# Four graph layers on one core: tokens four to a partition, the adjacency from ScalarE's queue, its square right behind the branch

## The chip, the cores and the metric

The kernel runs on one NeuronCore of a Trainium2 chip. The time is that of one execution on the device, in microseconds; several executions are made and their median is compared. A profiled execution gives, beside its own time, a trace of every instruction on the engines: PE (TensorE, matrix products), DVE (VectorE), ACT (ScalarE), POOL (GpSimd) and SP (which here only issues transfers). PE's instructions write into eight PSUM banks, which the text calls banks; all other tiles of a graph lie in SBUF.

## The reference

There are B = 32 graphs of N = 512 tokens with D = 128 features, and one adjacency matrix of 512 x 512, whose entries are 0 or 1 in the inputs used. Four layers follow each other, each added to its input:

```
for layer in (L0, L1, L2, L3):
    h = relu(layernorm(x))
    x = x + layer(h, adj)

L0: x_h = elu(h Wi + bi); e_ij = sigmoid(tgt_i + src_j + be) * mask_ij
    mask = adj + 0.005 * (adj == 0)
    recv = elu([e x_h, x_h * rowsum(e)] Wn + bn);  [recv, x_h] Wm + bm
L1: five gated steps: m = adj h; z, r = sigmoid(...); c = tanh(...); h = (1-z) h + z c
L2: adj (h W) + bias
L3: sum over k of (adj^k h) W_k, k = 0..3 (the two adjacencies are the same matrix)
```

## The kernel before

A graph's x is held as 128 partitions by four chunks by 128 features: token c*128 + p lies in partition p, chunk c. The tiles that a product with features needs lie the other way, features in the partitions and 512 tokens along the free axis. Float32 products of 512 columns make two passes on PE; products with the adjacency use rounded (float32r) operands, with the token side split into a high and a low part.

The kernel has one prologue and two arms. The prologue loads the adjacency as four row tiles (`A_nat`, loaded at L377 by the helper `load`, whose line L352 the profile shows), and the first graphs (`load_graph`, L369). DVE looks for entries that are neither 0 nor 1 (L551), PE adds up what it found (L566), DVE turns it into an integer `other` (L571), every engine reads it (L1088) and branches (L1089). The inputs used lead to the binary arm, `arm(True)`; the other arm is for any adjacency.

In the prologue PE also transposes the adjacency (L560): bank jc gets the four blocks of column chunk jc, and all four row tiles are operands of each of these operations. In the binary arm ACT makes the layer 0 mask from the banks (L794), POOL compares the mask with 2 to get the rounded transposed adjacency `adjT` (L871), POOL rounds the row tiles into `nat` (L876), and PE makes the square from both (L882), due at 45, which ACT copies out (L887, `adj2T`). PE also makes a permuted adjacency `adjQ` (L920, copied at L923) for the steps of layer 1.

Layer 0 of the first four graphs starts in the prologue. For each: moments on DVE (L513 to L516), a power on POOL (L518), normalising on DVE (L533, graphs 0 to 3), transposes on PE (L410), a copy with relu on ACT (L597), the product with Wi (L481), elu with an exponential (L579) and a tanh (L486) on ACT and a relu on DVE (L584, graphs 0 to 3) or on ACT (L587, all others), two more DVE operations (L589, L591), message and score products (L619), a spread of scores over PE (L656). `aggregated` then forms four masked score tiles (ACT L680, DVE L683), multiplies them with the messages (L691), sums them (pair sums on DVE, L703, and products with ones, L481), multiplies with the node's own features (L732), and makes the products with Wn (L481) and Wm (L742), which is added to x (L501). From graph 4 on transposes go through DRAM (L422, L424, then L435, L440 or L459).

The order of the work is made by a planner at build time. Each operation is listed by `op` with an engine, an assumed duration, a due time and its operands. `Plan.order` steps through time and lets each engine take the ready operation with the earliest due time, if buffers are free; the instructions are then issued in that order, engine by engine. While PE has nothing to do in the first stretch, the planner puts in a filler, a product of ones with ones into a spare bank (L339):

```
plan.idle = Op("PE", 0.224, 0.0, lambda: nc.tensor.matmul(
    spare[:, :P], at(ones), at(ones), start=True, stop=True), False, 0)
plan.idle.known, plan.fill = 0.4, FILL
```

`BRANCH` is the planner's time at which the prologue ends. `nudge` shifts due times by random amounts from a list of seeds, `HEAD_NUDGES`, for operations due before 130. Transfers go out from SP's queue, with the exceptions of accumulating ones from POOL (L719) and the last stores from ACT (L1037).

Of the kernel before, what the change touches and what calls it, by code (L numbers as in the profile page):

```python
# [17 lines left out]
P = 128  # L18
# [6 lines left out]
HEAD_NUDGES = (4000001, 4000006, 4000008, 4000034, 4000054, 4000088, 4000124, 4000206, 4000298, 4000710, 4000778,  # L25
    4000852, 4001301, 4001728, 4002027, 4002029, 4002137, 4002150, 4002536)
# [221 lines left out]
def tile_four_graph_layers(  # L248
# [36 lines left out]
    BRANCH, FILL = 10.0, 50.0  # L285
    MARGIN = 10.0
    FIRST = 4
    ONES = 0

# [26 lines left out]
    def at(v):  # L316
        if v.tile is not None:
            return v.tile
        return places[v.kind][v.slot] if v.whole is None else at(v.whole)[:, v.part]
# [3 lines left out]
    def const(name, shape, dt=F32):  # L323
        if name not in const_tiles:
            const_tiles[name] = cpool.tile(shape, dt, tag=name, name=name)
        return Val(tile=const_tiles[name])

    def chunks(t):
        return t.rearrange("p (c d) -> p c d", c=NC)
# [21 lines left out]
    def load(v, src, due, us=0.5, to=None, earliest=0.0, result=None):  # L351
        op("SP", us, due, lambda: nc.sync.dma_start(at(v) if to is None else to(at(v)), src), [], [v],  # L352
           earliest=earliest, result=result)
        return v
# [13 lines left out]
    def load_graph(b, due, result=None):  # L368
        op("SP", 0.48, due, lambda: nc.sync.dma_start(  # L369
            at(X[b]), x[b].rearrange("(c p) d -> p c d", p=P)),  # L370
            [], [X_group[b // G], X[b]] if b % G == 0 else [X[b]], result=result)
# [4 lines left out]
    for ic, v in enumerate(A_nat):  # L376
        load(v, adj[ts(ic, P), :], -9.5, 0.48, result=2.7 + 0.25 * ic)  # L377
    Wi_sb = load_const(Wi, [P, P], "Wi_sb", -9)
    bi_sb = load_column(bi, "bi_sb", -9)
    load_graph(1, -8.5, 3.2)  # L380
    load_graph(2, -8, 4.0)
# [35 lines left out]
    def by_qci(t):  # L417
        return t.rearrange("p (c q i) -> p q c i", c=NC, i=32)
# [136 lines left out]
    A_turned = [Val("b") for _ in range(NC)]  # L555
    for jc, pt in enumerate(A_turned):
        pt.pieces = True
        def turn(jc=jc, pt=pt):
            for ic in range(NC):
                nc.tensor.transpose(at(pt)[:, ts(ic, P)], at(A_nat[ic])[:, ts(jc, P)], at(ident))  # L560
        op("PE", T_TR, 8, turn, [*A_nat, ident], [pt])
# [39 lines left out]
    def scored(b, hT, due):  # L601
        KEEP = 12
        if b >= G:
# [4 lines left out]
                  relu_by_vector=b < FIRST)  # L608
# [150 lines left out]
    crossing = [*A_turned, *A_nat, *(v for x in begun for v in x[:4])]  # L759
# [13 lines left out]
    def arm(binary):  # L773
        with ExitStack() as stack:
            pool = stack.enter_context(tc.tile_pool(name=f"arm{binary:d}", bufs=1))
            plan.back_to(common)
            plan.slack = 0.3
            plan.free["b"].append((FILL, len(places["b"]) - 1))
            list_rest(binary, pool)
            plan.complete = True  # L780
            if not binary:
                issue(plan.order())
                return
            plan.nudge(0.0, 130.0, HEAD_NUDGES)
            order = plan.order(end=HEAD)
            plan.nudge(TAIL, 2000.0, TAIL_NUDGES)
            issue(order + plan.order())

    def list_rest(binary, pool):
        for v in crossing:  # L790
            v.left -= 1
        for jc, pt in enumerate(A_turned):
            def masked(jc=jc, pt=pt):
                nc.scalar.activation(at(mask)[:, jc, :], at(pt), AF.Identity,  # L794
                                     bias=at(ones)[:, :1], scale=1 / ALPHA - 1)
            if binary:
                op("ACT", T_COPY, 9 + jc, masked, [pt, ones], [mask])
                continue
            z = Val("f")
            op("ACT", T_COPY, 9 + jc, lambda z=z, pt=pt: nc.scalar.mul(at(z), at(pt), 1 / ALPHA), [pt], [z])  # L800
            op("DVE", T_VEC, 9 + jc, lambda jc=jc, z=z, pt=pt: nc.vector.scalar_tensor_tensor(
                at(mask)[:, jc, :], at(pt), 0.0, at(z), op0=ALU.is_equal, op1=ALU.add),
                [pt, z], [mask])
        for b in range(G):
            aggregated(b, begun[b], begin(b))
# [59 lines left out]
        for v in A_nat:  # L865
            if not binary:
                plan.free["f"].append((BRANCH, v.slot))
        if binary:
            adjT = Val(tile=pool.tile([P, NC, N], F32R, tag="AT", name="AT"))
            for jc in range(NC):  # L870
                op("POOL", 0.7, 22, lambda jc=jc: nc.gpsimd.tensor_scalar(  # L871
                    at(adjT)[:, jc, :], at(mask)[:, jc, :], 2.0, None, op0=ALU.is_gt), [mask], [adjT])
            adj2T = Val(tile=pool.tile([P, NC, N], F32R, tag="AA", name="AA"))
            nat = [Val("r") for _ in range(NC)]
            for kc in range(NC):
                op("POOL", 0.62, 24, lambda kc=kc: nc.gpsimd.tensor_copy(  # L876
                    at(nat[kc]), at(A_nat[kc])), [A_nat[kc]], [nat[kc]], earliest=26.0)
            for jc in range(NC):
                pt = Val("b")
                def square(jc=jc, pt=pt):  # L880
                    for kc in range(NC):
                        nc.tensor.matmul(  # L882
                            at(pt), at(nat[kc])[:, ts(jc, P)], at(adjT)[:, kc, :],
                            start=kc == 0, stop=kc == NC - 1,
                        )
                op("PE", NC * T_PASS, 45, square, [*nat, adjT], [pt])
                op("ACT", T_COPY, 45, lambda jc=jc, pt=pt: nc.scalar.copy(  # L887
                    at(adj2T)[:, jc, :], at(pt)), [pt], [adj2T])
        else:
            adjT = Val(tile=pool.tile([P, NC, N], F32, tag="AT", name="AT"))  # L890
            for jc, pt in enumerate(A_turned):
                op("ACT", T_COPY, 9 + jc, lambda jc=jc, pt=pt: nc.scalar.copy(
                    at(adjT)[:, jc, :], at(pt)), [pt], [adjT])
# [24 lines left out]
        for jc in range(NC):  # L918
            pt = Val("b")
            op("PE", T_ADJ, 44, lambda jc=jc, pt=pt: nc.tensor.matmul(  # L920
                at(pt), at(swap), by_qci(at(adjT)[:, jc, :]), start=True, stop=True),
                [adjT, swap], [pt])
            op("ACT", T_COPY, 45, lambda jc=jc, pt=pt: nc.scalar.copy(  # L923
                at(adjQ)[:, jc, :], at(pt)), [pt], [adjQ])
# [104 lines left out]
        def finished(g, ic, pz, d):  # L1029
            xv = X[g * G : (g + 1) * G]  # L1030
            def x_part():
                return at(X_group[g])[:, :, ic, :]
# [3 lines left out]
            def store():  # L1036
                (nc.scalar if g == NG - 1 else nc.sync).dma_start(  # L1037
                    out[g * G : (g + 1) * G, ts(ic, P), :].rearrange("b p d -> p b d"), x_part())
# [52 lines left out]
    with branch.Else():  # L1091
# [4 lines left out]
        out[B - G :, N - P :, :].rearrange("b p d -> p b d"),  # L1096
# [36 lines left out]
```

## Time and profile before

| | |
|---|---|
| median of 3 runs | 1611.24 us (1609.75 to 1612.16) |
| the profiled execution's own time | 1609.89 us |
| its span, first to last instruction | 1608.1 us |
| PE busy | 1599.2 us (99%), 6341 matmul records |
| DVE busy | 1405.8 us (87%) |
| ACT busy | 1120.9 us (70%) |
| POOL busy | 248.0 us (15%) |
| chain that ended last | PE 96% of the span |
| transfers | 188.01 MB, mean 117 GB/s |

A group's line in the profile names the source line, engine, operation, tiles (out<-in), shape and count. In a timeline a row has its start, its length, what it is and how often it follows itself; square brackets tell how long the engine idled before it and what released it. In a table of windows the first number behind the window is its length, and then come each engine's busy time and count, PE's granted clock, the share of the DMA engines and GB/s. A float32 product is two records in the profile (two passes). A busy PE is not always computing at its peak, since the ends of its records are modelled, and a filler counts as busy.

### The profile page before, as it was taken

What the parts mean: (1) busy time and instruction counts of PE and PEld (TensorE: products, weight loads), DVE (VectorE), ACT (ScalarE), POOL (GpSimd) and SP (SyncE); (2) the same over time, 40 slices, a digit from 0 to 9 for tenths busy, and PEclk for the clock granted to TensorE, in tenths of its full rate; (3) what the DMA queues carried; (4) which work ended last, traced back from release to release, by engine and by line L of the source; (5) the groups of instructions that cost most, each with busy time, mean ns of one, the idle gap of its engine ahead of it and who ended that gap; (6) DMA issues with size and microseconds to landing.
All of it is one profiled execution on the core that took longest, in us unless ns stands there. A gap on an engine that the chain in (4) does not pass through costs nothing.

```text
span 1608.1 us, 20921 instructions
## 1 busy us (share of the span) xinstructions
PE 1599.2 (99%) x6341; PEld 1026.2 (64%) x6341; DVE 1405.8 (87%) x3316; ACT 1120.9 (70%) x2119; POOL 248.0 (15%) x248
## 2 busy tenths in 40 slices
PE   9999999999999999999999999999999999999998
PEld 6655555666666666666666666666666666656687
DVE  8899999999898899888898898888998889888862
ACT  5877767886866767667776677676787676665661
POOL 5121011211211111111111111111111101100010
PEclk9999999999999999999999999999999999999999
DMA  3354445444453355453455534454544445333221
GB/s 96 90 148 131 127 111 134 110 123 127 132 149 108 106 125 139 125 135 109 106 138 131 136 94 125 118 145 125 132 127 121 134 116 129 92 92 98 86 60 49
DMA packets 284923, 188.01 MB, mean 117 GB/s; under 512 B 77312, under 2 KB 237952, under 8 KB 284800
## 3 DMA queue, kind: packets, MB, share of 16 engines
q1 hardware_dynamic: 270688, 162.98, 34.3%
q0 software_dynamic: 12528, 22.81, 8.4%
q8 instruction: 52, 0.85, 0.2%
q10 hardware_dynamic: 1584, 0.79, 0.2%
q14 instruction: 71, 0.58, 0.1%
HBM read 82.78 MB, written 73.33 MB: 97 GB/s over the span
## 4 chain that ended last, share of the span: by engine, by line
PE 96%; DVE 1%; DMA 1%; ACT 1%; SPq 0%; issue 0%; POOL 0%; DVEq 0%; ACTq 0%; POOLq 0%
PE b L481 45%; PE b L932 25%; PE b L1007 7%; PE b L691 7%; PE b L1016 4%; PE b L742 4%; PE b L995 2%; PE b L619 2%; PE b L729 1%; DMA f<-m 1%; DMA f<-in_adj_dram 0%; SPq L352 0%; ACT f L527 0%; PE b L882 0%; PE b L410 0%
## 5 line engine op out<-in xcount | busy, mean ns | idle before, releaser
L470 ACT COPY f<-b 128x512 f32<-128x512 f32 x388 | 223.2, 584 | 154.6 <-PE b L932 102.3
L518 POOL TENSOR_TENSOR s<-s,nhalf 128x4 f32<-128x4 f32 x128 | 154.4, 1206 | 975.9 <-DVE s L516 791.4
L932 PE MATMUL b<-AQ,r 128*128 128x512 f32 x1024 | 304.2, 439 | 0.0
L932 PEld LDWEIGHTS b<-AQ,r 128*128 128x128 f32 x1024 | 192.1, 188 | 89.5 <-issue 47.8
L957 DVE TENSOR_TENSOR f<-f,b 128x512 f32<-128x512 f32 x320 | 213.3, 678 | 29.9 <-PE b L481 23.8
L422 DVE STREAM_TRANSPOSE f<-f 128x512 f32<-128x512 f32 x246 | 207.8, 847 | 30.3 <-ACT f L527 29.2
L527 ACT ACTIVATE f<-x,s 128x128 f32<-128x128 f32 x496 | 203.8, 486 | 28.6 <-DVE s L522 28.2
L932 PE MATMUL b<-AT,r 128*128 128x512 f32 x768 | 220.3, 429 | 0.0
L486 ACT ACTIVATE f<-f,b4w 128x512 f32<-128x512 f32 x160 | 115.8, 724 | 118.2 <-DVE f L957 113.5
L932 PEld LDWEIGHTS b<-AT,r 128*128 128x128 f32 x768 | 144.0, 188 | 58.8 <-issue 25.3
L906 DVE TENSOR_TENSOR r<-f,r 128x512 fp32r<-128x512 f32 x224 | 152.3, 682 | 19.2 <-ACT r L902 18.9
L481 PE MATMUL b<-f,u5T 128*128 128x512 f32 x320 | 163.0, 593 | 0.6 <-DVE f L964 0.6
L481 PE MATMUL b<-f,u3T 128*128 128x512 f32 x320 | 163.4, 592 | 0.0
L481 PE MATMUL b<-f,w4T 128*128 128x512 f32 x320 | 163.1, 592 | 0.0
L481 PE MATMUL b<-f,w3T 128*128 128x512 f32 x320 | 163.1, 592 | 0.0
L481 PE MATMUL b<-f,w5T 128*128 128x512 f32 x320 | 162.7, 592 | 0.0
L902 ACT CAST r<-f 128x512 fp32r<-128x512 f32 x224 | 137.7, 619 | 18.5 <-DMA f<-m 18.0
L486 ACT ACTIVATE f<-b,b5w 128x512 f32<-128x512 f32 x160 | 109.3, 684 | 48.9 <-PE b L481 46.5
L486 ACT ACTIVATE f<-f,b3w 128x512 f32<-128x512 f32 x160 | 115.2, 721 | 34.5 <-DVE f L957 33.6
L974 DVE TENSOR_TENSOR f<-f,f 128x512 f32<-128x512 f32 x160 | 109.0, 682 | 28.8 <-ACT f L486 28.7
L1007 PEld LDWEIGHTS b<-V,f 128*128 128x128 f32 x1024 | 122.6, 192 | 15.1 <-issue 12.9
L719 POOL DMA_DIRECT2D f<-f x87 | 77.8, 894 | 344.7 <-DVE f L957 37.3
(114 smaller groups left out, 2379.1 us busy)
## 6 DMA issues: line engine op xcount, KB each, us to landing
m<-f SPq DMA_DIRECT2D x246, 256.0 KB, 2.2
f<-m SPq DMA_DIRECT2D x186, 256.0 KB, 2.9
f<-f POOLq DMA_DIRECT2D x87, 256.0 KB, 3.6
f<-m SPq DMA_DIRECT2D x240, 64.0 KB, 2.4
x<-in_x_dram SPq DMA_DIRECT2D x32, 256.0 KB, 3.3
f<-f SPq DMA_DIRECT2D x29, 256.0 KB, 2.3
f<-d SPq DMA_DIRECT2D x28, 256.0 KB, 5.6
out_dram<-x SPq DMA_DIRECT2D x28, 256.0 KB, 2.4
```

The lines of the kernel that those rows point to most:

```text
L422: op("DVE", us, due, lambda: nc.vector.transpose(view_out(at(blocks)), view_in(at(src))), [src], [blocks])
L470: op("ACT", us, due, lambda: nc.scalar.copy(at(t), at(src)), [src], [t])
L481: nc.tensor.matmul(to, at(w), of, start=start, stop=stop)
L486: op("ACT", us, due, lambda: nc.scalar.activation(at(dst), at(src), AF.Tanh, bias=at(bias), scale=scale), [src, bias], [dst])
L518: op("POOL", 1.2, due, lambda: nc.gpsimd.tensor_tensor(stat(SCALE), stat(VAR), at(neg_half), op=ALU.pow), [s, neg_half], [s], two=False)
L527: nc.scalar.activation(at(h)[:, ts(c, P)], at(X[b])[:, c, :], AF.Relu, bias=stat(SHIFT)[:, c : c + 1], scale=stat(SCALE)[:, c : c + 1],)
L691: op("PE", T_MM, d, lambda jc=jc: nc.tensor.matmul(at(pn), at(msg)[:, ts(jc, P)], at(es[jc]), start=jc == 0, stop=False), [msg, es[jc]], [pn])
L902: op("ACT", T_COPY, due, lambda: nc.scalar.copy(part(hi), whole()), [src], [hi], keep=1)
L906: op("DVE", T_VEC, due, lambda: nc.vector.tensor_tensor(part(lo), whole(), part(hi).bitcast(F32), op=ALU.subtract), [src, hi], [lo], two=two)
L932: nc.tensor.matmul(at(pa), at(part)[:, ts(jc, P)], view(at(columns)[:, jc, :]), start=jc == n == 0, stop=jc == NC - 1 and n == PARTS - 1,)
L957: op("DVE", T_VEC, d, lambda: nc.vector.tensor_tensor(at(s), at(u), at(pg), op=ALU.add), [u, pg], [s])
L1007: nc.tensor.matmul(at(pz)[:, ts(i, D)], at(t[i])[:, ts(ic, P)], at(V[k]), start=i == n == 0, stop=last and i == G - 1 and n == len(terms) - 1,
```

## The change

Tokens are placed four to a partition: token 4p + c lies in partition p, chunk c. The loads of x read 2048 contiguous bytes a partition instead of four pieces of 512; the stores of the result write pieces of 512 bytes, 2048 apart. Row tile c of the adjacency is rows 4p + c, and its columns are taken with stride 4 (`by_token`) wherever a chunk of columns is read. Sums over tokens, the mask and the squares are in the same new order throughout.

The adjacency's four loads are issued by ACT ahead of its table load. Each row tile is now transposed as soon as it is there, into all four banks (`adjacency_turned`), ahead of the branch. ACT rounds the row tiles into `nat` (four `q` buffers) and copies the banks into the rounded `adj_r`, also ahead of the branch; the mask comes from `adj_r` behind it. POOL's eight operations (L871, L876) are gone. The 16 matmuls of the square are listed one by one, due at 12, and so are planned right behind the branch. Relu of graphs 2 and 3 goes from DVE to ACT. `BRANCH` is 9, the planner adds 0.3 (PE) or 0.75 (others) for the branch itself, and there is a new list of nudges. The other arm transposes the adjacency again for itself.

```diff
-    BRANCH, FILL = 10.0, 50.0
+    BRANCH, FILL = 9.0, 50.0
+    SQUARE, NAT = 12.0, 0.0
+    BRANCHES = 0.75
+    A_LANDS = (3.0, 3.3, 3.6, 3.8)
...
-            at(X[b]), x[b].rearrange("(c p) d -> p c d", p=P)),
+            at(X[b]), x[b].rearrange("(p c) d -> p c d", c=NC)),
...
-        load(v, adj[ts(ic, P), :], -9.5, 0.48, result=2.7 + 0.25 * ic)
+        load(v, adj.rearrange("(p c) n -> c p n", c=NC)[ic], -9.5, 0.45, result=A_LANDS[ic], eng="ACT")
...
-        op("PE", T_TR, 8, turn, [*A_nat, ident], [pt])
+    def by_token(v):
+        return at(v).rearrange("p (t c) -> p c t", c=NC)
+
+    def adjacency_turned(due):
+        banks = [Val("b") for _ in range(NC)]
+        for pt in banks:
+            pt.pieces = True
+        for ic in range(NC):
+            def turn(ic=ic):
+                for jc, pt in enumerate(banks):
+                    nc.tensor.transpose(at(pt)[:, ts(ic, P)], by_token(A_nat[ic])[:, jc, :], at(ident))
+            op("PE", T_TR, due + ic, turn, [A_nat[ic], ident], banks)
+        return banks
+
+    adj_r = const("adj_r", [P, NC, N], F32R)
...
+    nat = [Val("q") for _ in range(NC)]
+    for jc, pt in enumerate(adjacency_turned(-1)):
+        op("ACT", T_COPY, NAT + jc, lambda jc=jc: nc.scalar.copy(chunks(at(nat[jc])), by_token(A_nat[jc])), [A_nat[jc]], [nat[jc]])
+        op("ACT", T_COPY, jc, lambda jc=jc, pt=pt: nc.scalar.copy(at(adj_rows[jc]), at(pt)),
+           [pt], [adj_rows[jc], adj_r])
...
-                  relu_by_vector=b < FIRST)
+                  relu_by_vector=b < 2)
...
-                op("POOL", 0.7, 22, lambda jc=jc: nc.gpsimd.tensor_scalar(
-                    at(adjT)[:, jc, :], at(mask)[:, jc, :], 2.0, None, op0=ALU.is_gt), [mask], [adjT])
...
-                op("POOL", 0.62, 24, lambda kc=kc: nc.gpsimd.tensor_copy(
-                    at(nat[kc]), at(A_nat[kc])), [A_nat[kc]], [nat[kc]], earliest=26.0)
...
-                op("PE", NC * T_PASS, 45, square, [*nat, adjT], [pt])
...
+            for n in range(NC * NC):
+                kc, jc = divmod(n, NC) if SPLIT else divmod(n, NC)[::-1]
+                op("PE", T_PASS, SQUARE, lambda jc=jc, kc=kc, pt=squares[jc]: nc.tensor.matmul(
+                    at(pt), at(nat[kc])[:, ts(jc, P)], at(rows[kc]), start=kc == 0, stop=kc == NC - 1),
+                    [nat[kc], rows[kc]], [squares[jc]])
...
-                    out[g * G : (g + 1) * G, ts(ic, P), :].rearrange("b p d -> p b d"), x_part())
+                    out[g * G : (g + 1) * G].rearrange("b (p c) d -> c p b d", c=NC)[ic], x_part())
```

## The prediction

> **What bounds the kernel now.** I read the page first, then the windows, then the timelines and the chain of the first 40 us. The page gives PE 1599.2 of 1608.1 us busy, and the chain puts 96% on PE. The windows show where PE is not busy, and how near DVE comes to it:
>
> ```profile
> core 0: us, PE busy (x) PEld busy (x) DVE busy (x) ACT busy (x) POOL busy (x), PEclk, DMA share, GB/s
> 0.00:10.00 10.00, 8.33 (x59) 7.69 (x59) 5.71 (x26) 1.68 (x3) 2.64 (x10) 1.00 0.77 219
> 10.00:20.00 10.00, 8.94 (x63) 7.15 (x62) 8.14 (x39) 7.40 (x13) 8.67 (x10) 1.00 0.53 138
> 20.00:30.00 10.00, 9.99 (x53) 6.46 (x52) 9.97 (x27) 6.72 (x16) 7.81 (x11) 1.00 0.10 26
> 30.00:40.00 10.00, 9.82 (x41) 5.69 (x40) 9.12 (x29) 7.14 (x15) 1.39 (x1) 1.00 0.01 2
> 40.00:130.00 90.00, 90.00 (x354) 55.37 (x353) 80.51 (x182) 71.22 (x138) 19.34 (x23) 1.00 0.44 116
> 130.00:400.00 270.00, 270.00 (x944) 162.06 (x943) 255.46 (x588) 202.93 (x379) 38.46 (x37) 1.00 0.45 124
> ```
>
> From 40 us on PE never stops, so time can be won only before. There it idles 1.67 + 1.06 + 0.01 + 0.18 = 2.92 us, and much of what counts as busy is the filler matmul of L339, which computes nothing. Windows of L339 alone:
>
> ```profile
> core 0: us, PE busy (x) PEld busy (x), PEclk, DMA share, GB/s
> 0.00:12.00 12.00, 6.73 (x40) 6.54 (x41) 1.00 0.72 202
> 12.00:20.00 8.00, 3.34 (x30) 3.17 (x29) 1.00 0.54 143
> 20.00:30.00 10.00, 3.03 (x22) 2.64 (x22) 1.00 0.10 26
> ```
>
> Filler 13.10 us and idle 2.92 us: PE loses 16.0 us of its first 40. The timelines say what it waits for (PE, then DVE, then POOL):
>
> ```profile
> 6.31 0.42 PE L560 MATMUL b<-ident,f 128*128 128x128 f32 x2
> 7.06 0.33 PE L560 MATMUL b<-ident,f 128*128 128x128 f32 x1 [0.33 <-DMA f<-in_adj_dram]
> 7.69 1.64 PE L560 MATMUL b<-ident,f 128*128 128x128 f32 x13 [0.30 <-DMA f<-in_adj_dram]
> ...
> 11.42 3.06 PE L339 MATMUL b<-ones 128*128 128x128 f32 x26
> ...
> 17.95 0.33 PE L825 MATMUL b<-ident,f 128*128 128x128 f32 x1 [1.06 <-DMA b4u<-in_L_gnn_u_b_dram]
> ```
>
> ```profile
> 24.03 1.89 DVE L683 SCALAR_TENSOR_TENSOR f<-f,mask 128x512 f32<-128x512 f32 x3
> 25.84 1.09 DVE L703 TENSOR_TENSOR f<-f,f 128x512 f32<-128x512 f32 x1
> ...
> 26.99 0.96 DVE L683 SCALAR_TENSOR_TENSOR f<-f,mask 128x512 f32<-128x512 f32 x1
> ```
>
> ```profile
> 25.57 3.87 POOL L876 CAST r<-f 128x512 fp32r<-128x512 f32 x4
> ```
>
> The adjacency tiles land one by one to 7.65; then comes the branch, then a filler stretch; from 20 us DVE is full. Under POOL's casts one DVE operation takes 0.96 to 1.09 instead of the 0.63 between the three at 24.03.
>
> **The change, part by part.** PE's useful work is the same: in the binary arm the changed program has the same transposes, squares (16), permutations (4) and products. Fillers fall from 18 ahead of the branch and 26 behind it to 17 and 17. The last 2010 rows of PE's built order are equal in both, so the end of the run is untouched. The sum is therefore what PE loses in its first 40 us.
>
> *Loads.* Four adjacency loads leave SP (1.91 us of issuing) for ACT's queue and go out at 0.72 to 2.6 instead of 1.23 to 3.15. ACT's table load (1.28 us) and the warm-up stand behind them and end near 4.1, before ACT's first tile: hidden. Wi, bi and graph 1 go out 2 us earlier; graph 2 now waits in SP's queue for the first adjacency tile, graph 3 for the third, behind them bias and Wm loads. First users: DVE near 11.0 and 17; x loads land 2.8 to 5.1 us after their issue near 4.3 and 6.3, so both are covered. When does the last adjacency tile land? Low: 7.65 less 0.6 of earlier issue less the 256 KB of graph 0 no longer ahead in its queue (0.88 us at the 291 GB/s of 5 to 10 us): 6.1. High: all of x0, Wi, the adjacency and graph 1 (1.64 MB) before it on the curve of before (147 GB/s to 5 us, then 291): 8.1. I take the middle, 7.0, having no nearer row.
>
> *PE up to the branch.* Seven fillers (14 passes) at 0.208 (19 passes took 3.96 us up to 5 us): 1.04 to 3.95. Then four transposes per tile as it lands (13 took 1.64) and one filler, to 7.0. Idle there: 7.05 − 3.95 − 12 × 0.126 − 0.24 = 1.35. After the last transposes five fillers (to 8.6), the count, three fillers, the transposes of graph 0, one filler; the register read and compare (0.58) hides behind a filler of 0.2 where it hid behind a product before: 0.4 idle.
>
> *ACT ahead of the branch* has two times four new 512-column casts. Three of the strided ones fall between landings, the fourth ends 7.6, the four PSUM copies (0.545 each: three L923 took 1.64) end 9.85, and its branch 10.45 (11.36 before). Queued behind them is graph 0's copy (L597): 11.05, so its product starts at 11.75 instead of 10.51; graph 1's copy goes from 14.96 to 15.1. That cost is covered by the squares: all 16 (0.23 each, 3.7 us) now stand there instead of fillers, and leave 33.8 and 43.9, where PE had other work anyway. If the rounded tiles come late, that cover is gone and PE idles one for one. Strided reading has no ACT row; low 0.62 (L902, contiguous), high 0.62 × 1.18/0.668 = 1.09 (slowest over fastest of DVE's L422, which reads contiguous or with stride 4). At 1.09 the branch of ACT comes 1.15 later. I take 0.62, the row of the same engine.
>
> *POOL* loses 4 × 1.49 (L871) and 3.87 (L876): 9.8 us. Its powers for graphs 1 and 2 come about 1 us sooner, and DVE runs at 0.6 to 0.68 between 24 and 30. *DVE* loses two relus (0.66 each) to ACT (0.58 each, in its gaps).
>
> *DVE's chain*, from 7.0, by spacings in the timeline (moments 1.26, normalising 1.03, a 512-column operation 0.60 to 0.66): counts to 7.75, graph 0 normalised 8.85, branch 11.0, graph 1 normalised 13.35, relu 14.0, graph 2 normalised 16.35, then masks and pair sums of graph 0 from 21.6 to 25.2, and its own-sum product (L732) at 27.7 where before has 31.73. Normalising graph 3 (1.03) stood before it and now stands behind it: 3.0 ahead. PE by the built order meets these at 22.5 (first L691), 28.65 (Wn) and 33.9 (Wm), each 0.2 to 0.6 behind its operand; one wait of 0.3 at graph 3's transposes.
>
> *Sum on PE:* start 1.04; fillers 14 × 0.208 + 54 × 0.118 (26 took 3.06) = 9.3; tiles 1.35; branch 0.4; other waits and hops 0.6: 12.7 against 16.0. Three pair-sum products stretched 0.18 to 0.25 by the late DVE (1.04, 1.11 and 1.10 in the chain for 0.86) go as well: 0.5 net. Gain 3.3 + 0.5 = **3.8 us**. The L825 wait (1.06) is in the 16.0; the weights are issued 1.5 us sooner and needed at 16.1, about when they land.
>
> *Output rows* keep 512-byte pieces but lie apart. The last store took 3.1 us to land. Bounds: 0, and 0.7 (f<-m 2.9 against m<-f 2.2 us). I take 0, as the pieces keep their size. Loads of x in larger pieces and all other stores lie under a DMA share of 0.36 to 0.47.
>
> **A rule against the change.** The row first: L339 takes 0.208 us a pass up to 5 us and 0.118 after 11 us, while PEclk shows 1.00 throughout. The Trainium skill, "TensorE: Matmul & The Clock Gate", Part 1, says PE starts at half rate and is released only after a window of some 3.4 us of sustained work. The changed PE pauses between 4 and 7 us; by that rule it could stay slow to about 8.3, and transposes and five fillers would take up to 1.5 us more: gain 2.3. I keep the sum by the rows, because the pauses are short.
>
> The Trainium skill, "SBUF — State Buffer", section "Door 1: The DMA port swizzle", says that an access which goes to a new 16-byte line each time pays; stride-4 float32 reads do that. No row here shows it for PE or ACT.
>
> **Rivals.** (1) *The start does not move enough.* Last tile at 8.1 (1.1 lost) and strided casts at 1.09 (0.7 of the 1.15 passes the squares' slack): gain 2.0, 1609.2. For it: tiles spaced 0.63 with 0.95 or more DMA share; against it: no 512-byte pieces ahead of them. (2) *Slower: the new order between about 45 and 860 us puts PE behind a turned tile.* m<-f lands after 2.2 us and f<-m after 2.9; a trip that nothing covers costs 5.1. It decides once 7.0 us are lost, so one trip in full and part of another; two give 1607.4 + 10.2 = 1617.6. For it: DVE is 255.46 of 270 busy there, so late work is caught up slowly. Against it: PE idled 0 us from 40 to 400 and 0.65 from 400 to 800, and 14.5 us of DVE idle are left. (3) *More:* last tile at 6.1, no hops, rows as above: 0.9 + 0.6, and the stretched products in full (0.2): gain 5.5, 1605.7.
>
> **How the numbers follow.** The profiled execution took 1609.89 (span 1608.1, 1.8 around it), 1.35 below the median of 1611.24. Less 3.8: 1606.1 for such an execution, **1607.4** for a median. A measurement tells 0.2%, 3.2 us, from no change: faster is below 1608.0. Forecast with case (3): 0.62. Rival 1, within 0.2%: 0.24. Rival 2: 0.14. The forecast's own range is 1605 to 1608. The range asked for goes below case (3) by the 1.2 that runs spread about their median (1604.5). Above, it takes in rival 1 with the store's 0.7 and the casts' other 0.45 (1610.4), and a third of one uncovered trip (1.6): 1612. The rest of rival 2 stays out.
>
> **What the next profile would show.** Right: fillers x68 and some 9.3 us; last adjacency transposes near 7.1; Wi's first product near 11.8 among the squares; no POOL casts, and mask products on DVE at 0.6 to 0.7; L732's first near 27.7; PE without idle from 35 us; the last 0.7 ms alike. Wrong: transposes or casts of stride 4 twice as long; a last tile after 8; PE idle above 2 us between 45 and 860; a landing of the last store above 3.8 us.

## The result, and the profile after

| | before | after |
|---|---|---|
| median | 1611.34 us (1609.75 to 1613.97, 8 runs) | 1606.47 us (1605.23 to 1609.74, 8 runs) |
| the profiled execution's own time | 1609.89 us | 1605.48 us |
| its span | 1608.1 us | 1603.6 us |

The ratio is 0.997, with a 95% interval of 0.9959 to 0.9981: 4.9 us less, where 3.9 (1611.34 less the forecast 1607.4) was forecast. The profiled executions are 4.5 us of span apart.

The windows of the changed kernel, with the columns of the first table of before (length; PE, PE's weight loads, DVE, ACT, POOL busy; clock; DMA share; GB/s):

```profile
0.00:10.00 10.00, 7.77 (x51) 7.11 (x51) 5.04 (x22) 6.62 (x8) 3.21 (x12) 1.00 0.75 242
10.00:20.00 10.00, 10.00 (x59) 8.14 (x60) 8.18 (x37) 9.70 (x21) 3.24 (x6) 1.00 0.53 136
20.00:30.00 10.00, 9.80 (x43) 5.83 (x43) 9.93 (x33) 7.97 (x18) 3.37 (x4) 1.00 0.02 6
30.00:40.00 10.00, 10.00 (x65) 7.75 (x64) 9.86 (x28) 9.95 (x23) 1.11 (x1) 1.00 0.17 55
...
130.00:400.00 270.00, 270.00 (x946) 162.29 (x945) 254.54 (x585) 202.37 (x380) 39.99 (x36) 1.00 0.46 125
400.00:800.00 400.00, 400.00 (x1581) 256.65 (x1580) 360.18 (x858) 287.23 (x547) 62.82 (x58) 1.00 0.46 124
```

PE idles 2.23 us in the first 10 and 0.20 in the next 30; before it was 1.67 and 1.25. The wait of 1.06 for a bias of layer 1 is gone. ACT, which was 1.68 busy up to 10 us, is 6.62 busy there and 9.70 in the next ten: it carries the new casts. The fillers alone (L339 before is L347 here; PE and PE's weight loads):

```profile
0.00:12.00 12.00, 6.34 (x34) 5.62 (x34) 1.00 0.64 202
12.00:20.00 8.00, 0.75 (x6) 0.82 (x7) 1.00 0.64 168
20.00:30.00 10.00, 1.70 (x14) 1.50 (x13) 1.00 0.02 6
30.00:40.00 10.00, 2.44 (x16) 2.10 (x16) 1.00 0.17 55
```

They are 68 passes with 11.2 us of records, against 88 with 13.1 (the windows count a record that lies across a bound twice, so their counts add up to 70 and 92). Nearly all that went stood between 12 and 20 us (3.34 before, 0.75 now), where the square now is; new ones stand behind 30 us. The timeline of PE shows the exchange:

```profile
4.98 0.96 PE L574 MATMUL b<-ident,f 128*128 128x128 f32 x4 [0.58 <-DMA f<-in_adj_dram]
...
7.86 0.75 PE L574 MATMUL b<-ident,f 128*128 128x128 f32 x4 [0.61 <-DMA f<-in_adj_dram]
8.44 1.28 PE L347 MATMUL b<-ones 128*128 128x128 f32 x10
...
11.13 0.39 PE L347 MATMUL b<-ones 128*128 128x128 f32 x2
11.27 1.41 PE L906 MATMUL b<-adj_r,q 128*128 128x512 f32 x5
12.52 1.02 PE L490 MATMUL b<-f,Wi_sb 128*128 128x512 f32 x2
12.97 2.42 PE L906 MATMUL b<-adj_r,q 128*128 128x512 f32 x8
...
23.60 3.10 PE L715 MATMUL b<-f,f 128*128 128x512 f32 x6 [0.18 <-DVE f L707]
```

L906 is the square; its last three passes end at 16.4. The row at 11.13 also shows how a sum of records misleads: the group of two fillers is 0.39 long, but the next row starts 0.14 behind its start, since the modelled end of a pass lies over the start of the next. Short groups are overstated in this way. So the losses are counted below from one PE start to the next: a filler with its whole distance, every other pass with what it takes beyond its usual distance (0.228 for a pass with the adjacency, 0.429 for a 512-column float32 pass, 0.109 to 0.112 for 128 columns). The undisturbed work is 1576.5 us in every kernel here, so the losses make up the whole difference:

| profiled execution | median us | lost on PE in the first 50 us | later | behind the last start |
|---|---|---|---|---|
| before | 1611.3 | 17.0 | 9.0 | 5.6 |
| after | 1606.5 | 13.8 | 7.9 | 5.5 |
| e1_sp_queue | 1607.1 | 14.0 | 12.0 | 5.6 |
| e2_tokens_back | 1607.4 | 13.6 | 8.6 | 5.6 |
| e4_square_late | 1616.6 | 17.1 | 14.5 | 5.6 |
| e5_weights_strided | 1606.7 | 14.5 | 8.7 | 5.6 |
| e6_no_fill8 | 1605.6 | 13.1 | 8.7 | 5.6 |
| e8_no_fill8_weights | 1605.7 | 13.5 | 8.0 | 5.5 |
| e7_before_act_casts | 1612.3 | 16.7 | 10.3 | 5.5 |
| e9_no_nudges | 1610.5 | 16.6 | 9.6 | 5.6 |
| e10_before_no_nudges | 1616.8 | 17.9 | 11.9 | 5.6 |

Of the 4.5 us between the two profiled spans 3.2 lie in the first 50 us, 1.1 later and 0.1 at the end. By place, PE loses 3.8 us less between 10 and 20 us and 1.1 less between 20 and 30, but 0.4 more before 10 and 1.2 more between 30 and 40: part of what the square gave comes back as fillers where it used to stand. DVE and ACT of the changed kernel at the start:

```profile
22.77 2.49 DVE L707 SCALAR_TENSOR_TENSOR f<-f,mask 128x512 f32<-128x512 f32 x4
25.18 1.29 DVE L727 TENSOR_TENSOR f<-f,f 128x512 f32<-128x512 f32 x2
...
28.84 0.68 DVE L756 TENSOR_TENSOR f<-f,b 128x512 f32<-128x512 f32 x1
```

```profile
4.87 4.32 ACT L583 CAST q<-f 128x512 fp32r<-128x512 f32 x4 [0.74 <-DMA f<-in_adj_dram]
9.08 2.04 ACT L584 CAST adj_r<-b 128x512 fp32r<-128x512 f32 x4
11.33 0.60 ACT L621 ACTIVATE f<-b 128x512 f32<-128x512 f32 x1 [0.21 <-PE b L419]
```

The four strided casts take 4.32, or 1.08 each, and fill ACT without a gap from the first tile to 9.1, when the copies of the banks start. The product of the node's own features on DVE (L756, L732 before) starts at 28.84 where before has 31.73.

### The profile page after: what moved, and what is told of

Its sections match the earlier page's. It is cut to its first block, busy times and chain, and to the rows that moved or that the text cites. A ratio compares the mean times of both kernels' runs of the same rounds, so it can differ in the third digit from the quotient of the medians.

```text
span 1603.6 us, 20898 instructions
## 1 busy us (share of the span) xinstructions
PE 1596.1 (100%) x6321; PEld 1024.3 (64%) x6321; DVE 1404.7 (88%) x3314; ACT 1130.4 (70%) x2129; POOL 240.3 (15%) x240
## 4 chain that ended last, share of the span: by engine, by line
PE 99%; DMA 0%; DVE 0%; ACTq 0%; issue 0%
PE b L490 46%; PE b L950 26%; PE b L1025 7%; PE b L715 7%; PE b L1034 4%; PE b L766 4%; PE b L643 2%; PE b L1013 2%; PE b L753 1%; DMA f<-in_adj_dram 0%; PE b L419 0%; PE b L347 0%; PE b L906 0%; ACTq L361 0%; PE b L680 0%; DVE s L522 0%
## 5 line engine op out<-in xcount | busy, mean ns | idle before, releaser
L536 ACT ACTIVATE f<-x,s 128x128 f32<-128x128 f32 x496 | 203.8, 487 | 27.7 <-DVE s L531 27.3
L950 PE MATMUL b<-adj_r,r 128*128 128x512 f32 x768 | 220.8, 430 | 0.0
L950 PEld LDWEIGHTS b<-adj_r,r 128*128 128x128 f32 x768 | 143.8, 188 | 59.2 <-issue 27.3
L924 DVE TENSOR_TENSOR r<-f,r 128x512 fp32r<-128x512 f32 x224 | 152.5, 683 | 13.1 <-ACT r L920 12.7
L920 ACT CAST r<-f 128x512 fp32r<-128x512 f32 x224 | 137.7, 619 | 12.3 <-DMA f<-m 11.9
L1025 PEld LDWEIGHTS b<-V,f 128*128 128x128 f32 x1024 | 122.7, 192 | 14.8 <-issue 12.7
```

The costliest lines, as they stand in the source:

```text
L536: nc.scalar.activation(at(h)[:, ts(c, P)], at(X[b])[:, c, :], AF.Relu, bias=stat(SHIFT)[:, c : c + 1], scale=stat(SCALE)[:, c : c + 1],)
L920: op("ACT", T_COPY, due, lambda: nc.scalar.copy(part(hi), whole()), [src], [hi], keep=1)
L924: op("DVE", T_VEC, due, lambda: nc.vector.tensor_tensor(part(lo), whole(), part(hi).bitcast(F32), op=ALU.subtract), [src, hi], [lo], two=two)
L950: nc.tensor.matmul(at(pa), at(part)[:, ts(jc, P)], view(at(columns)[:, jc, :]), start=jc == n == 0, stop=jc == NC - 1 and n == PARTS - 1,)
L1025: nc.tensor.matmul(at(pz)[:, ts(i, D)], at(t[i])[:, ts(ic, P)], at(V[k]), start=i == n == 0, stop=last and i == G - 1 and n == len(terms) - 1,
```

## The experiments

Each is the changed kernel with one edit, or with two where the heading says so; two runs start from the kernel before, as their headings say. Times of the kernel before beside them: 1611.59 us (20 runs) for the first four, 1611.76 (21 runs) for the next four and 1612.47 (10 runs) for the last.

### The adjacency from SP's queue again

```diff
-        queue = nc.sync if eng == "SP" else nc.scalar
+        queue = nc.sync
```

> The changed kernel with its four adjacency loads issued from SP's queue, interleaved with x, Wi, bi; the order of PE, DVE and POOL is unchanged. Theory A (tiles arrive as fast as the transfer engines bring everything that was asked for, whichever queue asks): the last tile lands within 0.5 us of the 7.81 of the changed kernel, time within 1 us of it. Theory B (a queue of its own brings the adjacency earlier): the last tile, issued near 3.6 instead of 2.14, lands at 9 or later, and the time rises by 1 to 1.5 us.

Measured: 1607.07 us (1606.16 to 1609.98, 7 runs), ratio 0.9974 [0.9963, 0.9985]. The last tile's transposes on PE:

```profile
8.16 0.75 PE L574 MATMUL b<-ident,f 128*128 128x128 f32 x4 [0.75 <-DMA f<-in_adj_dram]
```

They start 0.3 us later than from ACT's queue (7.86), and the start loses 0.2 more. That is all that the queue does; the median is 0.6 above the changed kernel's, inside both intervals.

This profiled execution took 1609.93, though. Its later losses are 4.1 us above those of the changed kernel, and nearly all of them come from one wait, in an order that ran without it in the other program. The waits of PE, then windows around it (PE, its weight loads, DVE, ACT, POOL; clock; DMA share; GB/s):

```profile
PE b L490 <- DVE f L982: 2.3, 1, 2.3
```

```profile
526.00:528.50 2.50, 1.01 (x3) 0.53 (x4) 2.50 (x5) 1.20 (x2) 0.88 (x1) 1.00 0.81 133
528.50:532.00 3.50, 3.50 (x10) 2.73 (x9) 1.18 (x4) 3.22 (x8) 0.86 (x1) 0.51 0.83 212
```

PE waits 2.33 us for DVE, and then its granted clock is 0.51 over the next 3.5 us. The clock record itself has 0.5 from 528.58 to 531.99, 3.41 us. Of the run's times, 1608.26, 1609.93 and 1609.98 stand apart from the other four (1606.16 to 1607.07), and the changed kernel has one such time too (1609.74). The mean granted clock on record is 0.998 for that one and for the three longest of the next experiment (1610.31 to 1610.71), and 0.999 or 1.000 for all others of these two kernels; the long ones of this experiment have 0.999 and 1.000, like the short ones. So lost clock goes with some of them, and what made the others long is open.

### Tokens and tiles in the old order

```diff
-            at(X[b]), x[b].rearrange("(p c) d -> p c d", c=NC)),
+            at(X[b]), x[b].rearrange("(c p) d -> p c d", p=P)),
...
-        load(v, adj.rearrange("(p c) n -> c p n", c=NC)[ic], -9.5, 0.45, result=A_LANDS[ic], eng="ACT")
+        load(v, adj[ts(ic, P), :], -9.5, 0.45, result=A_LANDS[ic], eng="ACT")
...
-        return at(v).rearrange("p (t c) -> p c t", c=NC)
+        return at(v).rearrange("p (c t) -> p c t", c=NC)
...
-                    out[g * G : (g + 1) * G].rearrange("b (p c) d -> c p b d", c=NC)[ic], x_part())
+                    out[g * G : (g + 1) * G, ts(ic, P), :].rearrange("b p d -> p b d"), x_part())
```

The last store, written apart at the end, is changed in the same way.

> The changed kernel with tokens in the old order: x in pieces of 512 bytes again, no reading with stride 4, stores as before. The order of all engines is unchanged. Theory A (stride-4 reading is what ACT's casts of 1.08 us pay, and larger pieces of x earn nothing that shows): casts take 0.6, ACT's copy of graph 0 comes 0.5 to 1.5 us sooner than 11.33, time 0.3 to 1 us below the changed kernel. Theory B (the larger pieces bring the first tiles sooner, and lighter loads help through the run): casts 0.6, but the last tile lands after 8.5, time 1 us or more above the changed kernel.

Measured: 1607.43 us (1606.03 to 1610.71, 11 runs), ratio 0.9978 [0.9969, 0.9987]. On ACT:

```profile
7.64 0.62 ACT L583 CAST q<-f 128x512 fp32r<-128x512 f32 x1 [0.30 <-DMA f<-in_adj_dram]
...
11.04 0.60 ACT L621 ACTIVATE f<-b 128x512 f32<-128x512 f32 x1 [0.83 <-PE b L419]
```

A cast takes 0.62 again, and a warm transpose 0.109 us a pass instead of 0.120. The casts keep pace with the tiles, and ACT now waits 0.83 for PE's transposes of graph 0, so its copy comes only 0.29 sooner. The time is not lower (the interval holds the changed kernel's ratio). So the order of the tokens has a price in single instructions and none that can be measured in the sum; the larger pieces of the loads and the stores at a distance show no effect either (5.6 and 5.5 us behind the last start of PE).

### The square not before 33

```diff
-                    [nat[kc], rows[kc]], [squares[jc]])
+                    [nat[kc], rows[kc]], [squares[jc]], earliest=33.0)
```

> The changed kernel with the 16 matmuls of the square not allowed before the planner's 33 us; the planner fills the gap with fillers and orders the rest anew. Theory A (the gain is that the square, 3.7 us of PE, stands where fillers stood): PE's loss in the first 40 us rises from 13.7 to 16 to 17.5, time 2.5 to 3.7 us above the changed kernel, about as the kernel before. Theory B (the gain is the earlier start and the freer DVE; the square would be done in some other gap): time within 1 us of the changed kernel.

Measured: 1616.56 us (1615.3 to 1616.87, 7 runs), ratio 1.0029 [1.0018, 1.0041]. The fillers alone:

```profile
12.00:20.00 8.00, 3.26 (x26) 3.04 (x25) 1.00 0.51 143
```

Between 12 and 20 us there are 3.26 us of them again, as before the change, and the start loses 17.1 us: the whole gain of the start (3.2) is gone. So the square behind the branch is what it rests on. The time overshoots, since the planner then makes another order for what follows. The waits of PE that are longest behind 40 us:

```profile
PE b L715 <- DVE f L707: 1.7, 2, 1.3
...
PE b L950 <- DVE r L924: 1.0, 1, 1.0
...
PE b L766 <- DVE f L615: 1.0, 1, 1.0
```

The longest of L707's (1.3) is at 99 us, the other two at 1583 and 1364 us. PE loses 14.5 us behind 50 us instead of 7.9. The run therefore shows the head's worth by its place in the trace, not by its time.

### The stride on the weights of the square, not on ACT's cast

```diff
-        op("ACT", T_COPY, NAT + jc, lambda jc=jc: nc.scalar.copy(chunks(at(nat[jc])), by_token(A_nat[jc])), [A_nat[jc]], [nat[jc]])
+        op("ACT", T_COPY, NAT + jc, lambda jc=jc: nc.scalar.copy(at(nat[jc]), at(A_nat[jc])), [A_nat[jc]], [nat[jc]])
...
-                    at(pt), at(nat[kc])[:, ts(jc, P)], at(rows[kc]), start=kc == 0, stop=kc == NC - 1),
+                    at(pt), by_token(nat[kc])[:, jc, :], at(rows[kc]), start=kc == 0, stop=kc == NC - 1),
```

> The changed kernel with ACT's four casts of the adjacency reading in order, and stride 4 moved into PE's weight reads of the square; all orders unchanged. Theory A (stride 4 costs ACT 0.5 us a cast, and ACT ahead of the branch holds up graph 0): casts 0.6, ACT's copy of graph 0 0.4 to 1.2 us sooner than 11.33, time 0.3 to 1 us lower. Theory B (the landing and the branch hold it up, or weight reads pay instead): time the same within 0.3 us, or higher.

Measured: 1606.66 us (1605.98 to 1608.06, 6 runs), ratio 0.997 [0.9958, 0.9982]. The casts take 0.62, but PE is the later one now. PE, then ACT:

```profile
6.35 2.66 PE L574 MATMUL b<-ident,f 128*128 128x128 f32 x12
```

```profile
11.74 0.60 ACT L621 ACTIVATE f<-b 128x512 f32<-128x512 f32 x1 [1.16 <-PE b L419]
```

ACT waits 1.16 us for the transposes of graph 0 and copies them 0.4 later than in the changed kernel. In this execution PE's passes keep a distance of 0.213 up to 8.75, so twelve transposes take 2.66; and fillers stand ahead of L419. So this run alone doesn't tell what the slow cast costs. The changed kernel does: there too the copy waits for PE behind the slow casts, by 0.21 us, and without the stride (the second experiment) it came only 0.29 sooner.

The stride has its price at the new place too. The weight loads of the square, here and in the changed kernel:

```profile
L906 PEld LDWEIGHTS b<-adj_r,q x16: 307/310/329, 11.7 to 16.6; 128*128 128x128 f32 x16
```

```profile
L906 PEld LDWEIGHTS b<-adj_r,q x16: 187/188/192, 11.2 to 15.9; 128*128 128x128 f32 x16
```

A load takes 0.31 us for 0.19 (shortest, median and longest in ns), and the 16 passes take 4.58 us from start to start, where they took 4.29. That is 0.3 of the 0.7 us which the start loses more than in the changed kernel; the rest goes with the slow passes (0.213) up to 8.75.

### Without the fillers ahead of the branch

```diff
-    plan.idle = Op("PE", 0.224, 0.0, lambda: nc.tensor.matmul(
-        spare[:, :P], at(ones), at(ones), start=True, stop=True), False, 0)
+    fillers = []
+    def filler():
+        fillers.append(len(fillers))
+        if not 8 <= fillers[-1] < 16:
+            nc.tensor.matmul(spare[:, :P], at(ones), at(ones), start=True, stop=True)
+    plan.idle = Op("PE", 0.224, 0.0, filler, False, 0)
```

The plan is the same; the five fillers ahead of the count and the three ahead of graph 0's transposes aren't issued (lines move by 4).

> The changed kernel without the five fillers ahead of the count and the three ahead of graph 0's transposes; all else in the same order. Theory A (ACT's eight casts, which end at 11.1, hold up graph 0, the fillers only pass the time): graph 0's copy on ACT moves from 11.33 by 0.3 us at most, PE's loss stays within 0.4 of 13.8, time within 0.5 us of the changed kernel. Theory B (the fillers hold up the count, the branch and graph 0's transposes, 1.1 us each): DVE's branch and all behind it 0.5 to 1 us sooner, time 0.5 to 1 us lower. If PE then pauses long enough to stay at half rate, its passes are 0.21 beyond 9 us and the loss grows instead.

Measured: 1605.63 us (1605.43 to 1606.37, 5 runs), ratio 0.9963 [0.9949, 0.9977]. ACT, then DVE:

```profile
10.79 0.63 ACT L625 ACTIVATE f<-b 128x512 f32<-128x512 f32 x1
```

```profile
22.13 2.49 DVE L711 SCALAR_TENSOR_TENSOR f<-f,mask 128x512 f32<-128x512 f32 x4
...
28.21 0.68 DVE L760 TENSOR_TENSOR f<-f,b 128x512 f32<-128x512 f32 x1
```

Graph 0's copy is 0.54 sooner, and with it the masks (22.13 for 22.77) and the own-feature product (28.21 for 28.84): fillers ahead of the branch do delay what DVE does 12 us later (the last tile landed at 7.66 here, so up to 0.15 of it can be that). The start loses 13.1 instead of 13.8. The median is the lowest of all, 0.8 below the changed kernel's, but with overlapping intervals.

### Both of these

The two edits above together.

> The changed kernel without those eight fillers, and with ACT's casts reading in order (stride 4 in PE's weight reads). Theory A (casts and fillers hold up graph 0 together, so only both taken away show): graph 0's copy on ACT near 10.4 to 10.8 instead of 11.33, its product near 11.4, PE's loss 12.5 to 13.3, time 0.4 to 1.2 us below the changed kernel. Theory B (DVE, whose branch comes at 12, holds up all that counts): copy sooner, but the first mask product on DVE stays within 0.3 of 22.8 and the time within 0.3 us.

Measured: 1605.71 us (1604.68 to 1607.28, 5 runs), ratio 0.9963 [0.995, 0.9977]. PE, then ACT:

```profile
6.35 2.76 PE L578 MATMUL b<-ident,f 128*128 128x128 f32 x12
```

```profile
10.62 0.60 ACT L625 ACTIVATE f<-b 128x512 f32<-128x512 f32 x1
```

Nothing is added: with neither fillers nor slow casts in the way the copy is 0.17 sooner than without the fillers alone, and the start loses 13.5 instead of 13.1. The square with strided weights has 0.3 of this (4.62 us for 4.30); the rest goes with PE's passes, which kept the long distance of 0.213 up to 10.6 us in this execution (up to 6.9 in the other).

### The kernel before, with POOL's four row casts on ACT

```diff
-                op("POOL", 0.62, 24, lambda kc=kc: nc.gpsimd.tensor_copy(
+                op("POOL", 0.62, 24, lambda kc=kc: nc.scalar.copy(
```

The plan's order stays; only the engine that makes the cast differs.

> The kernel before with the four casts of POOL between 25.6 and 29.4 done by ACT, which idles there; all other orders unchanged. Theory A (POOL's casts slow DVE): the mask products and pair sums there take 0.6 to 0.7 instead of 0.96 to 1.09, the first L732 moves from 31.73 to 30.0 to 30.8, PE's loss from 17.0 to 16.0 to 16.7, time 0.3 to 1 us below the kernel before. Theory B (DVE is slow there for another reason): they stay at 0.9 or more and the time within 0.3 us.

Measured: 1612.29 us (1609.55 to 1613.04, 11 runs), ratio 0.9998 [0.9989, 1.0007]. DVE:

```profile
26.34 0.68 DVE L703 TENSOR_TENSOR f<-f,f 128x512 f32<-128x512 f32 x1
27.07 0.68 DVE L683 SCALAR_TENSOR_TENSOR f<-f,mask 128x512 f32<-128x512 f32 x1
...
30.84 0.68 DVE L732 TENSOR_TENSOR f<-f,b 128x512 f32<-128x512 f32 x1
```

The same operations took 0.96 to 1.09 while POOL cast. So the casts on POOL were what slowed DVE, and without them its chain is 0.9 sooner (30.84 for 31.73). PE gains by it where it meets DVE: between 24 and 37 us its passes other than fillers lose 0.28 us beyond their usual distances, where they lost 1.15. But in all the start loses 16.7 instead of 17.0, since in this execution the wait for the bias of layer 1 is 1.30 instead of 1.06 and the fillers take 0.3 more at the start. The median shows no gain.

### No list of nudges, in the changed kernel and in the one before

```diff
-HEAD_NUDGES = (7100000, 7100078, 7100153, 7100154, 7100740, 7100413, 7100768, 7100794, 7100559, 7100664, 7100595,
...
-    7100950, 7100955, 7100970, 7100973)
+HEAD_NUDGES = ()
```

> The changed kernel with an empty list of nudges; the planner orders the rest by itself. Theory A (the list earns time behind the head too: without it PE stalls that the changed kernel doesn't have): PE's loss in the first 50 us within 1.5 of 13.8, stalls after it 2 to 8 us more, time 2 to 9 us above. Theory B (only the head counts): time within 1.5 us of the changed kernel.

Measured: 1610.49 us (1609.91 to 1611.58, 10 runs), ratio 0.9994 [0.9985, 1.0003]. Without its own list the changed kernel takes as long as the one before with its list; the start loses 16.6, and 9.6 follow later. The list is worth 2.8 us in the start and 1.7 behind it. Neither of the two theories had put it there to that extent. What it doesn't tell is what the old structure takes without its list; the same edit on the kernel before:

> The kernel before, with its list of nudges emptied, as the changed kernel was run without its own (that took 1610.5 us; with the list 1606.5). It says what the structure of the change is worth when neither program has a searched order. Theory A: the structure gives the start its gain, and the lists only keep the order of each program clean; the kernel before loses some 4 us without its list too: 1614 to 1617 us, and the changed program is 4 us or more ahead list for list. Theory B: the structure is worth little by itself, and the new list found what the old one did not: 1611 to 1612 us, about the time with the list, and at most 1.5 us behind the changed program without nudges. In the profile, A has more than 17 us lost by PE in its first 50 us (before: 17.0; the changed program without nudges: 16.6) or new stalls behind 40 us; B has 17 us and no new stalls.

Measured: 1616.82 us (1613.57 to 1619.68, 6 runs), ratio 1.0031 [1.0019, 1.0043]. That is theory A: the old kernel also falls back without a list, by some 4.4 us, and list for list the change keeps its worth: 0.9994 over 1.0031 is 0.9963, some 6 us, where it is 0.997 with the lists. The start loses 17.9, later 11.9. The waits of PE, and a window (columns as above):

```profile
PE b L480 <- DMA f<-m: 2.6, 1, 2.6
PE b L480 <- DVE f L731: 1.1, 2, 0.8
```

```profile
1200.00:1500.00 300.00, 296.66 (x1090) 183.24 (x1089) 258.65 (x561) 200.90 (x367) 35.15 (x33) 1.00 0.39 106
```

The largest is a product that waits 2.6 us for a turned tile, the mechanism of rival 2, in another program. Without lists the start differs by only 1.2 us and what follows by 2.3 (in profiled executions, of which that of the kernel before was its fastest). By place, the changed program still loses far less between 10 and 20 us (1.3 against 6.4), but 4.4 between 30 and 50 where the other loses 0.3: without the list fillers stand in the place which the square left. How much of the change's gain is structure and how much is the search can't be split cleanly: each order decides both.

## Why the prediction was right, point by point

**Place and sign.** Right. The sum rested on PE's first 40 us, and 3.2 of 4.5 us lie there; putting the square back to 33 takes exactly them away.

**The sum on PE, 12.7 against 16.0.** This is the step that failed in its working. The 16.0 counts the old fillers by their records (13.10), which overlap; the 12.7 counts the new ones by their distance (0.208 and 0.118). By distance on both sides the fillers are 11.8 and 9.7 and the idle time 2.9 and 2.4: 14.7 against 12.1, a gain of 2.6 and not 3.3. The loss of before was overstated by 1.3; the loss of after was too, by 0.6. There the idle terms (1.04 + 1.35 + 0.4 + 0.6) came to 2.4 instead of 3.4, since the branch and the hops cost PE 0.2 and not 1.0, and the fillers, forecast as x68 and 9.3, came to x68, as said, and 9.7. All the waits of PE that the view of the changed kernel lists:

```profile
PE b L574 <- DMA f<-in_adj_dram: 1.2, 2, 0.6
PE b L347 <- DVE ones L342: 1.0, 1, 1.0
PE b L715 <- DVE f L707: 0.2, 1, 0.2
```

The pair-sum products, forecast at 0.5, are not stretched any more (four passes in 1.72 from 26.53); with all else that changed they make the rest of the 3.2 that the start gained, 0.6. The start in all: 3.8 forecast, 3.2 measured.

**Loads: "I take the middle, 7.0".** Wrong by 0.8, within its bounds. The tiles landed at 4.84, 5.56, 6.46 and 7.81, against 4.24, 6.36, 7.02 and 7.64 before, although they were issued 0.5 us sooner. The queue itself is worth 0.3 (8.11 from SP). In the first 10 us 2.42 MB are moved where it was 2.19, at a DMA share of 0.75 against 0.77; that the tiles share the engines with the earlier loads of Wi and graph 1 would fit, but no run took those away.

**ACT: "I take 0.62".** Wrong: 1.08, the upper bound (1.09). The lower end was chosen because it was the same engine's; the row with the same access, DVE's strided one (0.668 to 1.18), was the nearer. The Trainium skill, "SBUF — State Buffer", section "Door 1: The DMA port swizzle", says that each access which crosses to a new 16-byte line pays, and the runs agree: 1.08 against 0.62 for a cast, 0.310 against 0.188 for a weight load and 0.120 against 0.109 for a transpose pass. Graph 0's copy came at 11.33 (11.05 forecast) and the first Wi product at 12.52 (11.75).

**What a late ACT costs.** Rival 1 came nearly true in its conditions (last tile 7.81 of 8.1, cast 1.08 of 1.09) and not in its price (gain 2.0). It let 0.7 of the casts' lateness and 1.1 of the tiles' through to PE. The runs with fast casts gain nothing, because PE is itself not ready earlier: it has fillers, the count and graph 0's transposes ahead, up to 11.27, and from there its windows show 10.00 of 10.00 busy up to 20 us. (Without eight of these fillers the start loses 0.7 less.) The cover which the forecast named, the squares, held.

**DVE's chain.** The order and the durations are as forecast (0.62 to 0.64 an operation between 22.8 and 26.4, no POOL casts); the clock times are late by what ACT and PE passed on: masks at 22.77 (21.6), own features at 28.84 (27.7), first L715 at 23.60 (22.5), Wn at 30.00 (28.65), Wm at 34.97 (33.9). The fillers behind 30 us (2.44 us) don't come of this: they stand in the built order, and the forecast's x68 counts them. The run on the kernel before shows that the faster DVE frees PE of the stretched passes, by 0.9 us (the forecast had 0.5 net for three of them), but its median shows no gain.

**Rival 2.** It did not decide: the changed kernel shows no idle PE from 40 to 1200 us. But the price exists. Other orders lose 1.7 to 6.6 us more behind 50 us than the searched ones (e9, e10, e4), and in one execution of this same order (e1) a single wait took 2.3 us and half clock after it.

**Behind 50 us and the end.** The forecast had nothing here, and the end was as said: last store at no cost, 5.5 us behind the last start against 5.6, and much the same losses behind 1200 us. The 1.1 us in between were not foreseen. By distance, before loses 0.8 and 0.2 us at 436 and 439 us and 0.2 each at 980 and 988; only the first is a wait of any length (0.63). The forecast's "from 40 us on PE never stops" left these out, and the changed kernel has no wait there. As executions of one order differ by more than that, whether the change has a share in it stays open. It is this, not the start, that makes the measured gain larger than the forecast one.

**The clock.** The row-based choice held in the profiled execution: passes of 0.213 end at 5.67, not at 8.3. But that was luck, and the reason given ("the pauses are short") was not sound. In the clock's records of each of the eleven traces, the granted clock changes only at whole steps of 3.413 us: in the changed kernel full clock lasts 1597.44 us, 468 such steps, and in e1 it lasts 153 steps, then 1 at half clock and 315 again at full clock. This raster lies differently in each execution. Counted on it, the slow passes end in all eleven with the first step in which PE was busy for at least 0.83 of the time. The steps that hold the pause for the first tile, in the changed kernel and in e5:

```profile
2.26:5.67 3.41, 2.83 (x14) 2.56 (x14) 1.02 (x8) 2.29 (x3) 0.00 (x0) 1.00 0.96 320
```

```profile
1.93:5.34 3.41, 2.78 (x14) 2.51 (x14) 0.23 (x2) 1.91 (x3) 0.00 (x0) 1.00 0.84 287
```

The pause of 0.58 us in the changed kernel left 0.83 busy, and full clock came at its end. The pause of 0.63 in e5 left 0.81 (e8: 0.82), and the slow passes went on for one step more, to 8.75 and 10.61. The other eight steps that ended the slow passes were 0.84 to 1.00 busy, and they ended at 4.3 to 6.9. No run varied the pause by itself, so the bound between 0.82 and 0.83 is what these eleven show and no more. The Trainium skill, "TensorE: Matmul & The Clock Gate", Part 1, says that the window which releases the clock runs freely and isn't set by the kernel's start, which agrees, and that the point varies by some half a microsecond to either side; the spread here is wider, 6.3 us. The long distance up to 8.75 goes with a start that loses 0.7 us more (14.5 against 13.8), less the 0.3 of the strided weights.

## What to carry to other kernels

Where one engine is the bound, its loss can be counted exactly from the distances of its starts, and both sides of a comparison have to be counted that way: sums of records overstate short groups. Work that merely stands where fillers stood is free, and so are the slower instructions that prepare it, for as long as that cover lasts; find out what the cover is before pricing what is slow. What it is worth depends on what then fills the place it left. And when a planner makes the order, an edit's time also holds the luck of the new order, 4 us here on both sides, so judge the edit by where the trace loses time, and with the search left out on both sides.

## What the runs showed of the hardware

- A stall of 2.3 us on PE halved its granted clock for 3.41 us, 1.1 us after PE had resumed (e1, 528.58 to 531.99). A wait of 2.56 us in e10 was followed by 1.00. The raster tells them apart. In e1 the stall lies wholly in one step, and PE was busy for 1.09 of its 3.41 us; in e10 a bound at 1337.02 cuts the wait, and its two steps are 0.67 and 0.58 busy, the second the lowest of all steps that kept the clock:

```profile
525.17:528.58 3.41, 1.09 (x3) 0.61 (x4) 3.41 (x7) 1.82 (x3) 1.08 (x2) 1.00 0.69 113
```

```profile
1333.61:1337.02 3.41, 2.29 (x6) 0.74 (x4) 3.41 (x6) 2.35 (x5) 0.00 (x0) 1.00 0.53 135
1337.02:1340.44 3.42, 1.98 (x5) 1.03 (x6) 2.34 (x4) 2.10 (x4) 0.00 (x0) 1.00 0.70 257
```

The Trainium skill, "TensorE: Matmul & The Clock Gate", Part 1, has the clock fall back after an idle window of about 3.4 us; here a shorter pause was enough once, in a step that was not idle but 0.32 busy.
- In the table of windows the clock reads 1.00 for the first 5 us, while the passes keep a distance of 0.213 us, twice that of later. The slow start is read from distances, not from that column.
- With stride 4, ACT's 512-column cast of float32 takes 1.08 us and not 0.62; a weight load on PE takes 0.31 and not 0.19, most of it under the passes (16 of them 4.58 for 4.29); a 128-column transpose pass loses only a tenth (0.120 for 0.109).
